# A C2f block with attention on one core: a norm in halves, parameter work reordered, one product moved, a new tail order

## The chip, the cores and the metric

The kernel runs on one core of a Trainium2 chip. The metric is the device time of one execution in microseconds (us), and the time before is the median of three runs. All arithmetic is float32.

## The reference, cut to what matters

Eight images of 512 channels and 32x32 pixels are normalized by groups, and go through one block with a residual around it.

```python
x = x + block(group_norm(x))            # 32 groups of 16 channels

def block(x):                           # cbs = silu(batch_norm(conv(.)))
    t = cbs(x, cv1)                     # 1x1, 512 -> 512
    ys = [t[:, :256], t[:, 256:]]
    for i in range(2):
        z = cbs(ys[-1], m_cv1[i])       # 3x3, 256 -> 256
        q, k, v = qkv_i(z)              # 1x1, 4 heads of 64
        z = softmax(q @ (k + r_i) / 8) @ v        # 1024 x 1024 per head
        ys.append(ys[-1] + silu(batch_norm(m_cv2[i](z))))     # 1x1
    return cbs(concat(ys), cv2)         # 1x1, 1024 -> 512
```

## The kernel before, in words

**Engines.** TensorE (PE) multiplies, ScalarE (ACT) applies functions and copies, VectorE (DVE) adds, GpSimd (POOL) does small work and issues part of the DMAs, SyncE (SP) issues the rest. Channels lie on the 128 partitions, so an image is four tiles of 128x1024 at the input and two in the inner steps. A product of 128x512 is recorded as two matmul instructions.

**Pairs.** Images are handled in four pairs (p = 0 to 3), and each pair runs in this order: the first 3x3 convolution for both images; projection and attention of image a with the weights of n = 0; m2, which is the 1x1 convolution behind the attention; projection and attention of image b; the second convolution for both; the same attentions with n = 1; and cv2, which joins all parts. While a pair is in its first two attentions, the next pair's images a and b are normalized (`group_norm`), and their cv1 is begun behind each attention (`next_cv1`: begin, go_on, sums, rest). In pair 0 the next cv1 is done directly (`direct`), with one(0) in begin, one(1) in go_on, and one(2) and one(3) in rest. In pairs 1 and 2 it is done by Strassen's scheme with seven products; rest(0) to rest(3) are four of them, made from sums t1 to t4 of the normalized input, which lie in the tiles of q and k.

**The 3x3 convolution** is done by Winograd's scheme. `tiles_in` turns an input into the tiles v on DVE (with two small memsets of w_rows on POOL in each of three passes), `conv3x3` multiplies these by filters u and turns the products back on DVE. `make_u` turns nine taps of the weights into one third of the filters in each of three groups: six DVE operations (L408 to L413) and two on ACT (L406, L407), and ahead of two groups three sums on DVE (L390 to L396). It is a generator with eight steps per filter, so that its caller can place steps between other work; each group ends with three stores to DRAM from POOL (L417). The tiles u_new come from a ring of ten slots of the tag u, which also holds loaded weights. The filters of n = 0 are made at the start, those of n = 1 in and behind the attention of the first image of pair 0: (0,0) inside it, then (0,1), (1,0) and (1,1). Their taps were all read into the tiles Y2[0] and Y2[1].

**Attention** (`attention_fast`): for each of four groups (two heads times half the queries), eight blocks of keys. l_ps (L957) are the logits, pt (L961) their exponentials on ACT, acc (L975, L977) their sum on DVE, av_ps (L991) the product with v. Two blocks make a slot; `behind` holds what is issued behind slot (g, at), where plain g stands for (g, 0), `NG` for the end of the last group, and NG + 1 for what follows it. `hooks` fills it: a step of the norm where the slot is in NORM_A (image a) or NORM_B (image b), a filter step where its number is in `us`. The sums of exp are inverted to scale the output. Usually they go through DRAM to be turned and spread (`sums`, `spread`, `scale`). With `at_once` the last group's are kept in PSUM by `last_sums` (L1025), inverted on DVE over 128x512 (L1108), and only a check goes through DRAM.

**The group norm** takes statistics (L653, L654), averages them over groups on PE (`gn_mean`: gm, dev; `gn_rstd`: gr, L679), makes gr and shift on POOL (L680, L736, L737) and applies them on ACT (L741), one whole tile at a step. The first pair's norms are `group_norm_part`, with the statistics on ACT for the later ones (L694, L721).

**Parameter work on POOL.** `make_r` sums the two position vectors into r_new (L206) and stores it (L210), `make_sq` makes the Strassen sums of the projection weights on DVE and stores seven blocks from POOL (L237), `keep_y` stores the cv1 output (L1439, L1440). For n = 1 make_r and make_sq are asked for behind slots (1, 2) and (3, 2) of the first attention.

**Order.** The order in the program isn't the order on an engine. A planner in the framework places each instruction in its engine's queue by its own costs when its inputs and buffers are there, and so may bring it far forward. `with tc.issue_after(i)` sets the instructions of its block that run on the engine of i behind i, and has no effect on other engines. PSUM has three accumulators of the tag `big` and one of `av`.

**The tail.** The last image ends with `cv2`: half of its products were made earlier (`parts`), DVE adds the new half (L1415), ACT applies silu (L460), DVE adds the input x_res (L1418), and the result is stored (L1420).

## Time and profile before

| | us |
|---|---|
| median of three runs (2348.94 to 2358.16) | 2351.87 |
| profiled execution, its own time | 2352.97 |
| its span | 2351.5 |
| PE busy in the span | 2231.2 |
| DVE busy | 1745.9 |
| ACT busy | 1085.3 |
| POOL busy | 229.6 |
| PE's mean granted clock | 0.987 |

All times in the profile count from the span's start. Busy time says how long an engine had an instruction in work, not that the work was needed then. A gap before an instruction is written as [us <- what ended it]; a wait for several things is put down to the last of them. Slices or stretches of the span show which engine is the bound there.

### The profile page before, as it was taken

How to read it: one execution, taken by the hardware profiler on the slowest of the kernel's cores; microseconds unless marked ns; L12 is line 12 of the kernel's file. 1: busy time of each engine (PE TensorE's matmuls, PEld its weight loads, DVE VectorE, ACT ScalarE, POOL GpSimd, SP SyncE). 2: the span in 40 equal slices, each digit the busy share in tenths (PEclk: the TensorE clock that was granted, in tenths of full speed). 3: DMA queues.
4: the chain of work that ended last, by engine and by line, in shares of the span. 5: the costliest groups of instructions: out<-in, count | busy, mean ns of one | idle time of the engine just before them, and what ended most of it. 6: DMA issues, size and time to landing. Idle time of an engine off the chain costs nothing.

```text
span 2351.5 us, 40448 instructions
## 1 busy us (share of the span) xinstructions
PE 2231.2 (95%) x16338; PEld 1083.4 (46%) x16338; DVE 1745.9 (74%) x2630; ACT 1085.3 (46%) x1321; POOL 229.6 (10%) x426
## 2 busy tenths in 40 slices
PE   7798899999999999999999999999999999999997
PEld 3553336533456343744347443564344733473443
DVE  6978677858938778986866868887794867786642
ACT  7245362546224665355422575545622454335532
POOL 4302200010020000000022000000002000000002
PEclk9899899999999999999999999999999999999998
DMA  9522715331266042612158132442126611151114
GB/s 330 205 76 100 286 37 195 126 118 46 69 184 220 25 166 66 213 59 91 38 134 257 60 117 88 131 158 73 55 64 172 225 43 59 59 192 37 51 32 127
DMA packets 128068, 281.31 MB, mean 120 GB/s; under 512 B 34144, under 2 KB 55376, under 8 KB 126848
## 3 DMA queue, kind: packets, MB, share of 16 engines
q1 hardware_dynamic: 99888, 192.50, 24.9%
q0 software_dynamic: 27984, 86.13, 12.0%
q8 instruction: 131, 2.15, 0.4%
q14 instruction: 65, 0.53, 0.1%
HBM read 210.55 MB, written 68.03 MB: 118 GB/s over the span
## 4 chain that ended last, share of the span: by engine, by line
PE 58%; issue 16%; DVE 14%; DMA 4%; ACT 2%; POOL 1%; SPq 0%; DVEq 0%; ACTq 0%; POOLq 0%
PE av_ps L991 13%; PE l_ps L957 12%; PE c L1209 7%; PE c_new L1209 5%; PE m_ps L1189 4%; PE p_ps L847 4%; PE ps L486 3%; PE c_ps L603 3%; PE x_ps L1309 3%; DVE acc L977 2%; PE pv_ps L853 2%; ACT pt L961 1%; PE s_ps L1008 1%; DMA rs<-r_dram 1%; DVE c_e L611 1%
## 5 line engine op out<-in xcount | busy, mean ns | idle before, releaser
L961 ACT ACTIVATE pt<-l_ps 128x1024 f32<-128x1024 f32 x512 | 495.6, 1023 | 348.9 <-PE l_ps L957 316.0
L977 DVE TENSOR_TENSOR acc<-acc,pt 128x1024 f32<-128x1024 f32 x384 | 471.5, 1228 | 91.9 <-ACT pt L961 68.5
L957 PE MATMUL l_ps<-q,kr 64*64 64x512 f32 x4096 | 491.2, 593 | 14.9 <-ACT pt L961 12.4
L991 PE MATMUL av_ps<-pt,vT 64*64 64x512 f32 x4096 | 488.7, 594 | 8.5 <-DVE z L999 7.5
L957 PEld LDWEIGHTS l_ps<-q,kr 64*64 64x64 f32 x4096 | 157.0, 133 | 288.3 <-issue 247.1
L991 PEld LDWEIGHTS av_ps<-pt,vT 64*64 64x64 f32 x4096 | 155.2, 134 | 285.4 <-issue 240.8
L603 PE MATMUL c_ps<-v_in,u 128*64 128x128 f32 x4320 | 240.2, 273 | 5.5 <-issue 5.5
L603 PEld LDWEIGHTS c_ps<-v_in,u 128*64 128x64 f32 x4320 | 235.8, 137 | 13.4 <-issue 13.4
L1189 PE MATMUL m_ps<-z,m_sb 128*128 128x512 f32 x256 | 114.6, 600 | 4.6 <-DVE z L1063 4.6
L847 PE MATMUL p_ps<-t_z,sq 128*128 128x512 f32 x224 | 106.7, 597 | 7.9 <-DVE c_t L610 7.9
L975 DVE TENSOR_TENSOR acc<-pt 128x1024 f32<-128x1024 f32 x64 | 79.0, 1234 | 37.2 <-ACT pt L961 37.1
L608 ACT COPY c_m<-c_ps 128x512 f32<-128x512 f32 x48 | 28.1, 585 | 168.9 <-PE c_ps L603 101.6
L460 ACT ACTIVATE t<-m_ps,bh,sh 128x512 f32<-128x512 f32 x64 | 46.8, 775 | 93.1 <-PE m_ps L1189 85.5
L847 PE MATMUL p_ps<-z,sq 128*128 128x512 f32 x168 | 80.2, 604 | 8.2 <-ACT z L460 8.2
L1259 POOL DMA_DIRECT2D c_out<-in_x_dram x56 | 50.5, 996 | 303.2 <-ACT c_out L460 301.3
L1189 PEld LDWEIGHTS m_ps<-z,m_sb 128*128 128x128 f32 x256 | 48.7, 192 | 65.1 <-issue 55.3
L521 POOL MEMSET w_rows<- 128x32 f32 x48 | 7.8, 163 | 679.1 <-PE s_ps L1008 389.8
L1063 DVE TENSOR_TENSOR z<-z,rs 128x512 f32<-128x512 f32 x64 | 43.9, 686 | 33.9 <-DMA rs<-r_dram 33.8
L486 PE MATMUL ps<-x,w 128*128 128x512 f32 x128 | 57.8, 606 | 5.9 <-ACT y_half L460 5.9
L999 DVE TENSOR_TENSOR z<-av_ps,z 128x512 f32<-128x512 f32 x64 | 43.9, 686 | 23.7 <-ACT z L998 23.7
L460 ACT ACTIVATE z<-z,bh,sh 128x512 f32<-128x512 f32 x64 | 46.9, 802 | 30.9 <-DVE z L641 29.8
L460 ACT ACTIVATE c_out<-cz,bh,sh 128x512 f32<-128x512 f32 x14 | 16.7, 1293 | 91.3 <-DVE cz L1286 91.3
(308 smaller groups left out, 3193.2 us busy)
## 6 DMA issues: line engine op xcount, KB each, us to landing
u<-u SPq DMA_DIRECT2D x135, 512.0 KB
sq<-sq SPq DMA_DIRECT2D x42, 384.0 KB
rs<-r_dram SPq DMA_DIRECT2D x120, 128.0 KB
x<-in_x_dram SPq DMA_DIRECT2D x28, 512.0 KB
r_in<-r SPq DMA_DIRECT2D x28, 512.0 KB
y_in<-y SPq DMA_DIRECT2D x28, 512.0 KB
c_out<-in_x_dram POOLq DMA_DIRECT2D x56, 256.0 KB, 5.4
out_dram<-c_out POOLq DMA_DIRECT2D x56, 256.0 KB, 3.6
```

The source lines that it names most:

```text
L460: silued[0] = nc.scalar.activation(dst, src, AF.Silu, scale=sh[:, k : k + 1], bias=bh[:, k : k + 1])
L486: last_product[0] = nc.tensor.matmul(ps[:, half, :], w_of(k), rhs_of(k, half), start=(k == begin), stop=(k == end))
L603: nc.tensor.matmul(to[o], us[cp][:, k, row, c, o], rhs, start=(k == 0), stop=(k == NM - 1),)
L847: nc.tensor.matmul(ps[:, o, :], w[:, o, :], rhs, start=not onto, stop=True, skip_group_check=onto)
L957: nc.tensor.matmul(ps[kh * HD : (kh + 1) * HD, hd, :], kr[r, c, o : o + HD], q[r, c, ts(half, HALF)], start=True, stop=True,)
L961: last_exp[0] = exp = nc.scalar.activation(pt, ps, AF.Exp, scale=SCALE)
L975: return nc.vector.tensor_tensor(accs[g], pt[0], pt[1], ALU.add)
L977: ins = nc.vector.tensor_tensor(accs[g], accs[g], pt[i], ALU.add)
L991: nc.tensor.matmul(avs[g][hd * HD : (hd + 1) * HD, kh, :], vT[r, j, o : o + HD], pt[i][r, hd, :], start=(j == 0), stop=(j == NJ - 1),)
L1189: nc.tensor.matmul(pss[oc][:, half, :], m2_sb[:, n, k, ts(oc, P)], ao[:, k, ts(half, HALF)], start=(k == 0), stop=(k == NM - 1),)
L1209: nc.tensor.matmul(ps[:, o, :], w[:, k, ts(o, P)], rhs[part][:, c], start=(k == 0 and not onto), stop=(k == KB - 1), skip_group_check=onto,)
L1309: nc.tensor.matmul(ps[:, o, :], w[:, c, ts(o, P)], rhs[c], start=(c == 0 and not onto), stop=(c == 1), skip_group_check=onto,)
```

## The change

The change edits eight places.

1. `group_norm` takes `pieces` and applies the norm to parts of a tile; image b of a pair uses 2 and a new list of slots, NORM_B. It also records the POOL instruction that makes the shift (`shifted`).
2. At the start two filter steps move behind the mean of the first image's second half, four steps instead of five stand before the second image's mean, and the later filter stores and `keep_y(0)` are set behind the second image's shift on POOL.
3. In the first attention, make_r and make_sq for n = 1 are set behind the shift of the third image on POOL, make_r one slot group later; the steps of the first filter are at other slots.
4. That attention runs with `at_once`, and go_on of the next cv1 is issued from inside it.
5. The taps of filter (0,1) are read early into Y2[1], those of (1,0) and (1,1) into tiles of the tags q and k. Sixteen filter steps are set behind the scaling on DVE, and the rest stays behind m2.
6. In pairs 1 and 2 the sum t4 of image b is in p4 and not in the tile of k, and rest(3) is issued behind the second convolution.
7. In `cv2` all the sums of a channel block are issued first, and the residual sum and store of a block are issued one block later.
8. `end.check` for the first attention follows its m2.

The diff, cut to its core:

```diff
-        def group_norm(xts):
+        def group_norm(xts, pieces=1):
...
-            nc.gpsimd.tensor_scalar(shift, shift, -1.0, None, ALU.mult)
+            shifted[0] = nc.gpsimd.tensor_scalar(shift, shift, -1.0, None, ALU.mult)
             yield
             for c in range(NX):
-                with tc.issue_after(last_exp[0].ins) if last_exp[0] else nullcontext():
-                    nc.scalar.activation(
-                        xts[c], xts[c], AF.Identity, scale=gr[:, c : c + 1], bias=shift[:, c : c + 1]
-                    )
-                yield
+                for half in range(pieces):
+                    part = xts[c][:, ts(half, HW // pieces)]
+                    with tc.issue_after(last_exp[0].ins) if last_exp[0] else nullcontext():
+                        nc.scalar.activation(
+                            part, part, AF.Identity, scale=gr[:, c : c + 1], bias=shift[:, c : c + 1]
+                        )
+                    yield
...
+            late, outs = [], []
+
+            def out_later(t, size, q, rows, has):
+                def run():
+                    with tc.issue_after(outs[-1].ins) if outs else nullcontext():
+                        outs.append(nc.vector.tensor_tensor(t, t, has[:, :size], ALU.add))
+                    q.dma_start(rows, t)
+                    residual()
+
+                return run
...
+                        added = nc.vector.tensor_tensor(part, src, part, ALU.add)
                         src = part
+                        if n == 0 and late:
+                            with tc.issue_after(added.ins):
+                                flush(1 if final else 0)
+                    srcs.append((at, size, src))
+                with tc.issue_after(added.ins) if final else nullcontext():
+                    flush()
+                for n, (at, size, src) in enumerate(srcs):
...
                     silu(from_planes(t), by_slot(src), bn_cv2 + oc)
-                    nc.vector.tensor_tensor(t, t, res[done][:, :size], ALU.add)
                     q = nc.sync if final else nc.gpsimd
-                    q.dma_start(rows_of(out, oc, at, size), t)
+                    late.append(out_later(t, size, q, rows_of(out, oc, at, size), res[done]))
...
-        chunk = make_u(0, 0, 1, areas[0, 0, 1], first_units)
-        for _ in range(2):
-            made = next(chunk)
     first = begin(Y_ORDER[0], [0])
     with tc.issue_after(first.ins), tc.issue_after(made.ins):
         averaged = next(norm)
+    chunk = make_u(0, 0, 1, areas[0, 0, 1], first_units)
+    with tc.issue_after(averaged.ins):
+        for _ in range(2):
+            made = next(chunk)
...
-    with tc.issue_after(averaged.ins), tc.issue_after(shifted.ins):
+    with tc.issue_after(made.ins), tc.issue_after(shifted.ins):
         nc.vector.tensor_scalar(rstd, bnp[:, :, 3], BN_EPS, None, ALU.add)
...
     with tc.issue_after(made.ins):
-        for _ in range(5):
+        for _ in range(4):
             made = next(chunk)
...
-    with tc.issue_after(averaged.ins):
+    with tc.issue_after(averaged.ins), tc.issue_after(shifted.ins):
         for made in chunk:
             pass
...
-    keep_y(0, y0s, Y1[0])
+    with tc.issue_after(shifted.ins):
+        keep_y(0, y0s, Y1[0])
...
+        def t_qk_p():
+            if len(pairs_of_t) == 1:
+                pairs_of_t.clear()
+                return held("p4")
+            return t_qk()
...
-            f = s.strassen_cv1(take_blocks("sw", None, which, SW_NAMES), xts, y0s, y1, t_qk)
+            f = s.strassen_cv1(take_blocks("sw", None, which, SW_NAMES), xts, y0s, y1, t_qk_p if which else t_qk)
...
         def filters(keys):
-            for oc, k, at in keys:
-                yield from make_u(1, oc, k, load_raw(1, oc, k, Y2[at]))
+            for oc, k, area in keys:
+                yield from make_u(1, oc, k, area)
+
+        def load_late(oc, k, area):
+            nc.gpsimd.dma_start(
+                area[:, : 9 * P].rearrange("p (t o) -> p t o", o=P), m_cv1_w[1, ts(k, P), :, ts(oc, P)]
+            )
+            return area
+
+        def late_area(tag):
+            return act.tile([P, 2 * HW], F32, tag=tag, name="taps_late")
...
-        NORM_B = ((0, 2), (0, 3), (1, 2), (1, 3), 2, (2, 1), (2, 2), (2, 3))
+        NORM_B = ((0, 1), (0, 2), (0, 3), (1, 1), 2, (2, 1), (2, 2), (2, 3), 3, (3, 1), (3, 2), (3, 3))
         if p == 0:
-            more_u = filters([(0, 0, 0)])
-        behind = hooks(NORM_A, range(0, 16, 2)) | {NG: begin_cv1(0, Y1[0], ia + 2)}
+            more_u = filters([(0, 0, load_late(0, 0, inside(Y2[0])))])
+            second_taps = load_late(0, 1, inside(Y2[1]))
+        behind = hooks(NORM_A, (0, 1, 4, 10, 11, 12, 13, 14)) | {NG: begin_cv1(0, Y1[0], ia + 2)}
...
+            def with_r():
+                with tc.issue_after(s.shifted[0].ins):
+                    make_r(1, raw_1)
+                first()
+
+            behind[2, 1] = with_r
+
+            def with_sq():
+                before()
+                with tc.issue_after(s.shifted[0].ins):
+                    make_sq(1, q_tiles, [t[:, j] for t in q_sums for j in range(2)])
+
+            behind[3, 2] = with_sq
+        if p == 0:
+            behind[NG + 1] = lambda: nxt.go_on()
+        end = s.attention_fast(qkv, z[:, :, 0], at_of(ia, 0), behind, at_once=p == 0)
...
-                more_u = filters([(0, 1, 1), (1, 0, 1), (1, 1, 1)])
-                end.sums()
-                nxt.go_on()
-                end.spread()
-                with tc.issue_after(end.added.ins):
-                    for _ in range(5):
-                        made = step_u()
-                with tc.issue_after(made.ins):
-                    end.scale()
-                    for _ in range(7):
+                more_u = filters(
+                    [(0, 1, second_taps)] + [(1, k, load_late(1, k, late_area(tag))) for k, tag in enumerate("qk")]
+                )
+                with tc.issue_after(end.scaled.ins):
+                    for _ in range(16):
                         made = step_u()
                 last = m2_a()
-                with tc.issue_after(made.ins):
-                    for _ in range(3):
-                        made = step_u()
+                end.check()
...
-            norm = s.group_norm(xs)
+            norm = s.group_norm(xs, 2)
...
-            for i in range(4):
+            for i in range(4 if direct else 3):
                 nxt.rest(i)
...
         t = s.conv3x3(1, vs, u_of(1), z, summed=z[:, :, 0])
+        if more and not direct:
+            nxt.rest(3)
```

More of the change, by code (lines that the diff above doesn't have):

```diff
@@ L463, in silu @@
             return silued[0]
+        shifted = [None]
         silu_in, last_product, silued, last_exp, m2_silu = [], [None], [None], [None], [None]
@@ L1404, in cv2, with flush @@
             done = 0
+            late, outs = [], []
[6 more added lines that the diff above has]
+                return run
+            def flush(n=0):
+                while len(late) > n:
+                    late.pop(0)()
             for oc in range(NO):
@@ L1407, in cv2 @@
                 ps = cv2_products(w_of, rhs_of, oc, ks, ends=(ks[0], ks[-1]), by_half=oc == NO - 1)
+                final = parts and oc == NO - 1
+                srcs = []
+                added = None
                 for n, size in enumerate(sizes(oc)):
-                    _, at, _ = places[done]
-                    final = parts and oc == NO - 1
-                    t = act.tile([P, HALF], F32, tag=("h", "h", "rs")[n] if final else "h", name="t", bufs=4 if final and n == 2 else 2)[:, :size]
+                    at = sum(sizes(oc)[:n])
                     src = ps[:, at // HALF, at % HALF : at % HALF + size]
@@ L1414, in cv2 @@
                         part = parts[oc][:, at : at + size]
-                        nc.vector.tensor_tensor(part, src, part, ALU.add)
+                        added = nc.vector.tensor_tensor(part, src, part, ALU.add)
                         src = part
+                        if n == 0 and late:
[5 more added lines that the diff above has]
+                for n, (at, size, src) in enumerate(srcs):
+                    tag = ("h", "h", "rs")[n] if final else "h"
+                    t = act.tile([P, HALF], F32, tag=tag, name="t", bufs=4 if tag == "rs" else 2)[:, :size]
                     silu(from_planes(t), by_slot(src), bn_cv2 + oc)
-                    nc.vector.tensor_tensor(t, t, res[done][:, :size], ALU.add)
                     q = nc.sync if final else nc.gpsimd
-                    q.dma_start(rows_of(out, oc, at, size), t)
+                    late.append(out_later(t, size, q, rows_of(out, oc, at, size), res[done]))
                     done += 1
-                    residual()
+                if not parts:
+                    flush()
+            flush()
         return SimpleNamespace(**locals())
@@ L1668 @@
             before = behind[3, 2]
-            first = behind[1, 2]
+            first = behind[2, 1]
             raw_1 = load_r(1)
-            behind[1, 2] = lambda: (first(), make_r(1, raw_1))
-            behind[3, 2] = lambda: (before(), make_sq(1, q_tiles, [t[:, j] for t in q_sums for j in range(2)]))
-        end = s.attention_fast(qkv, z[:, :, 0], at_of(ia, 0), behind)
+            def with_r():
[11 more added lines that the diff above has]
+        end = s.attention_fast(qkv, z[:, :, 0], at_of(ia, 0), behind, at_once=p == 0)
         for made in more_u:
```

## The prediction

> **What bounds the kernel now.** I read the page first, then busy times over chosen stretches, then the timeline wherever a stretch showed idle TensorE time. Page, sections 1 and 2:

> ```profile
> PE 2231.2 (95%) x16338; PEld 1083.4 (46%) x16338; DVE 1745.9 (74%) x2630; ACT 1085.3 (46%) x1321; POOL 229.6 (10%) x426
> PEclk9899899999999999999999999999999999999998
> ```

> TensorE (PE) is the bound: 95% busy, so all that can be had without removing matmuls is 2351.5 - 2231.2 = 120 us of idle time, plus what it loses at a lowered clock. The change removes no matmul of weight, so it is priced by gaps. Stretches (us; busy time of PE, PEld, DVE, ACT, POOL with counts; clock; DMA share; GB/s):

> ```profile
> 64.00:83.30 19.30, 15.26 (x38) 6.52 (x37) 14.84 (x29) 6.82 (x6) 15.85 (x16) 1.00 0.58 208
> 83.30:107.80 24.50, 12.50 (x162) 12.08 (x163) 24.19 (x50) 1.17 (x2) 1.78 (x8) 0.80 0.59 210
> 107.80:137.90 30.10, 29.10 (x426) 26.29 (x426) 29.92 (x60) 5.99 (x10) 0.55 (x1) 0.93 0.51 172
> 155.80:221.90 66.10, 59.81 (x546) 21.16 (x545) 52.43 (x76) 42.20 (x51) 6.67 (x12) 0.97 0.11 39
> 221.90:257.90 36.00, 25.52 (x62) 10.36 (x59) 23.27 (x56) 9.47 (x17) 17.31 (x29) 0.82 0.78 267
> 291.80:354.60 62.80, 58.15 (x546) 20.17 (x545) 48.00 (x60) 40.16 (x45) 4.04 (x8) 1.00 0.14 51
> 752.50:810.60 58.10, 57.63 (x546) 21.49 (x545) 49.68 (x65) 39.16 (x44) 3.68 (x5) 1.00 0.10 26
> 861.10:924.90 63.80, 58.44 (x546) 20.16 (x545) 56.01 (x75) 39.37 (x44) 4.04 (x8) 1.00 0.12 39
> ```

> The reader is to see three stages. From 83.3 to 137.9 (first convolution) VectorE (DVE) is busy 54.1 of 54.6 us: what delays DVE before it delays everything. From 221.9 to 257.9 (after the first attention) PE is idle 10.5 us at clock 0.82. And the second image's attention under which the next norm runs takes 62.8 us (pair 0) and 63.8 us (pair 1), against 58.1 us for the first image's in pair 1, with the same matmuls; pair 2's is 63.1.

> The timeline says what ends those waits. Before the first convolution:

> ```profile
> 55.72 2.80 DVE L408 TENSOR_TENSOR u_new<-taps 128x256 f32<-128x256 f32 x1 [2.15 <-DMA u<-u_new]
> 56.16 2.06 POOL L206 TENSOR_TENSOR r_new<-rw_sb,rh_sb 128x512 f32<-128x512 f32 x2
> 65.39 11.00 POOL L206 TENSOR_TENSOR r_new<-rw_sb,rh_sb 128x512 f32<-128x512 f32 x2
> 78.95 0.69 DVE L548 TENSOR_TENSOR w_d<-w_rows 128x512 f32<-128x512 f32 x1 [4.46 <-POOL w_rows L521]
> ```

> GpSimd (POOL) builds r_new here though the program asks for it in the first attention; a DVE operation of 0.42 us takes 2.80, and DVE waits 4.46 us for a memset queued behind r_new and four DMA issues. After the first attention:

> ```profile
> 247.68 2.08 PE L486 MATMUL ps<-x,w 128*128 128x512 f32 x2 [5.87 <-ACT y_half L460]
> 253.62 0.69 DVE L1063 TENSOR_TENSOR z<-z,rs 128x512 f32<-128x512 f32 x1 [3.08 <-DMA rs<-r_dram]
> 254.36 3.78 PE L1189 MATMUL m_ps<-z,m_sb 128*128 128x512 f32 x4 [4.60 <-DVE z L1063]
> ```

> m2 stops half way until the last softmax sums have gone through DRAM and back. And in the second image's attention (alike at 901 to 908 and 1460 to 1467):

> ```profile
> 331.27 0.15 DVE L679 TENSOR_SCALAR gr<-gv_ps 128x4 f32<-128x4 f32 x1
> 334.61 2.37 ACT L741 ACTIVATE x<-x,shift,gr 128x1024 f32<-128x1024 f32 x2 [5.02 <-POOL shift L737]
> 337.94 1.09 PE L957 MATMUL l_ps<-q,kr 64*64 64x512 f32 x8 [2.80 <-ACT pt L961]
> ```

> gr is read late, ScalarE (ACT) waits 5.02 us for the shift with an exponential queued behind, runs two whole-tile norms, and PE waits.

> [...]

> **Part A, start-up.** The parameter-sum blocks (make_r, make_sq) are tied behind the third image's shift on POOL, so four r_new, their four stores and the early sq stores leave 55 to 80 us. That takes away the 4.46 wait and the stretch, 2.80 - 0.42 = 2.4. Moving two filter steps behind the mean lets gm be copied when the first filter ends, about 21.4 instead of 23.05 (12 filter operations of 0.42 started every 0.34 had shared that time), and PE restarts 1.6 us sooner. The rstd wait of 2.1 us at 27.9 shrinks too. But filter buffers still wait for stores (3.3 us until 48.7, 2.2 until 55.7) with DMA at 0.81 to 1.05 of its time, and these waits take back early arrival: I count 1.1. One filter step fewer before the second image's mean and keep_y behind its shift take its norm forward from 50.6; PE ends the first image at 51.0 and had 0.48 us to wait, so nothing more. Sum 4.5 + 2.4 + 1.1 = **8 us off**, all on DVE's path. Bounds: 3 (the memset's wait alone, partly) and 11 (the store waits shrink as well).

> **Part B, first attention and after.** make_r now runs in the attention at (2,1): four r_new of 1.04 us, four stores of 0.55 us, then memsets and filter stores queued behind on POOL; seven sq issues follow at (3,2). DVE has 66.1 - 52.4 = 13.7 us free there, and filter steps leave slots 5 to 9, where the mean waited (2.0 us at 187). A blocked POOL costs up to 4 x 1 us of DVE: **0**, bounds 4 either way.

> After it, at_once replaces the trip through DRAM by eight s_ps matmuls (1.09 us at L1025), two row copies (0.57 each), an add (0.69), a reciprocal of 128x512 (3.35, L1108) and the scale (0.69). one(1) goes ahead as before. The second image of this pair already has this order: one(0) at 354.60, m2 done at 376.5, 22 us. Today's 36.0 become 22.0: 14 us. s_ps is done at 230, scaling at about 236, m2 starts near 237, so the reciprocal hides behind one(1) (7.1 us). The last-total DMA and its 0.16 us add hide behind m2.

> What comes next: all filter work of (0,1), (1,0), (1,1) is tied behind the scale. One filter takes 9.6 us of DVE (a group of 2.1, two of about 3.75), three 28.8, with four m2 sums of 0.69: 236 + 31.6 = 268. The last two lie in q and k, so kr can't be written earlier. Its product would be ready at 221.9 + 22 + 13.9 (two more products) + 3.4 = 261. PE goes on with q and v products in the other two accumulators for about 7 us (L817 takes 7.07 for all v), which covers most of it; I charge 3. The two raw loads (7.0 us landed at 233.9) start once logits have released q and k, some 14 us before needed. Ends: nothing charged, or 8 with DMA (0.78 and 0.80 now from 222 to 292) near full: **11 off**, bounds 14 and 6.

> **Part C, the norm by halves.** In three attentions rstd moves from (1,3) to (1,1): three slots of about 3.6 us before the first norm, where there was one. Eight norms of half a tile, one per slot (about 0.72 us each by L721), replace four of 1.24 in four slots; 8 x 0.72 - 4 x 1.24 = 0.8 us more on ACT, in slots with two exponentials of 0.97, so 2.7 of 3.6 us. At the 58.1 us of an attention with its norm in order: 4.7 + 5.7 + 5.0 = 15.4. But pair 1 already has 56.0 us of DVE work, 96% of 58.1, so not all: **11 off**, bounds 14 and 4.

> **Part D, one product behind the second convolution** (pairs 1 and 2). It takes 3.43 us of PE. That convolution is DVE's: from 944.3 to 997.3 DVE has no gap, PE waits 1.1 and 1.2 us at its end. DVE's work stays, so nothing is won; the product takes an accumulator that the next projection used, freed only at 994 to 995. t4 in p4 moves no work. **1 lost** in all, bounds 0 and 3.

> **Part E, the tail.** Sums of the parts no longer wait behind ACT; output adds come one channel block later. But silu waits for a buffer whose output DMA takes up to 5.9 us, and that remains:

> ```profile
> 2327.70 1.31 ACT L460 ACTIVATE t<-part,bh,sh 128x512 f32<-128x512 f32 x1 [11.14 <-DMA out_dram<-t]
> 2332.84 1.28 DVE L1415 TENSOR_TENSOR part<-ps,part 128x512 f32<-128x512 f32 x2
> ```

> Stepping the last four silus forward by these waits ends between 2339 and 2342.3, as now: **1 off**, bounds 3 off and 1 lost.

> **Sum**: -8 + 0 - 11 - 11 + 1 - 1 = -30 against the profiled execution's own 2352.97 (span 2351.5), so 2323; the median of the runs is 1.1 lower, hence 2322. All good ends give -46, all bad ends -5.

> **Rivals.** First: DVE becomes the bound where PE's gaps close. For: 96% in part C, 31.6 us of filters in one go. Against: today's gaps end on other engines. A gives 6, B 5, C 6, the rest 0: 17 off, 2335. Second: the norm change does little, because the gr read stays behind the tile transforms of g = 1 on DVE (it came after nine of them at 331.27). C gives 3, total 22 off: 2330. Third, slower: k is filled and read too late. The ring has ten slots, four held by weights, so two filter groups are in flight; if each group waits for its stores (4.7 us at start-up, issue 51.04, buffer taken 55.72) nine groups take 9 x (3.9 + 4.7) = 77 us and kr waits until 313, 49 us past the forecast's 264: 2371. It decides from 264 on: the gain is gone at 294. Against: at 261 to 273 groups ran through without such a wait.

> **Chances.** Forecast 0.69, first rival 0.16, second 0.09, third 0.06. A measurement of this kernel can tell about 0.5%, 12 us, from no change: faster means below 2340. The first rival straddles that a little: faster 0.87, same 0.07, slower 0.06. The range reaches from nearly all good ends (2304) past the first rival (2341).

> **What would show it.** No r_new before the first attention and no w_rows wait at 79; first attention starting near 148 instead of 155.8; 22 to 25 us from its end to m2's end, with clock near 1; a kr write that PE waits for less than 4 us; second images' attentions at 58 to 60 us without the 2.8 us gap; a convolution no shorter in pairs 1 and 2. An attention still at 63, or kr later than 20 us after m2, would make it wrong.

## The result, and the profile after

The changed kernel takes 2347.7 us (median of 13 runs, 2343.4 to 2351.9), the kernel before in the same comparison 2354.8 us (2348.9 to 2359.3). The ratio is 0.9968, with a 95% interval of 0.9958 to 0.9979: 7 us faster, where 30 were forecast, and outside the range. The profiled execution took 2349.4 us, its span is 2348.0 us, 3.5 less than before. Page of the changed kernel, sections 1 and 2:

```profile
PE 2237.3 (95%) x16338; PEld 1089.6 (46%) x16338; DVE 1748.5 (74%) x2632; ACT 1089.3 (46%) x1334; POOL 224.8 (10%) x426
PEclk9899999999999999999999999999999999999998
```

PE is busy 6 us longer with the same 16338 matmuls: idle time fell by almost 10 us, and most of that came back as busy time of the same matmuls. Part of it is the clock: the time at half clock, up to PE's last matmul, is 54.6 us in this profile and 47.8 in that of before. The clock's dip in the fifth slice, after the first attention, has gone; single stretches further on ran at 0.95 to 0.97, too short to show in a slice. Busy time over stretches of the changed kernel (us; PE, PEld, DVE, ACT, POOL with counts; clock; DMA share; GB/s). They are, in this order: from the first attention's end to the end of its m2; from there to the second image's attention; that attention in pair 0, in pair 1 and in pair 3:

```profile
219.30:241.40 22.10, 22.10 (x61) 9.51 (x58) 11.88 (x21) 6.22 (x7) 7.02 (x13) 1.00 0.57 186
241.40:281.00 39.60, 35.01 (x96) 17.61 (x94) 38.30 (x92) 16.83 (x29) 15.90 (x30) 1.00 0.91 333
281.00:343.30 62.30, 59.54 (x546) 21.42 (x545) 48.76 (x61) 41.11 (x49) 5.23 (x8) 0.97 0.24 88
850.10:913.00 62.90, 58.12 (x547) 21.09 (x545) 55.05 (x74) 40.11 (x48) 5.23 (x8) 1.00 0.13 43
1950.40:2016.10 65.70, 60.09 (x539) 20.30 (x538) 57.13 (x73) 35.19 (x40) 3.46 (x8) 0.97 0.16 55
```

The same view of the kernel before, for two stretches that the prediction did not look at, the one behind m2 and the second image's attention of pair 3:

```profile
258.10:291.80 33.70, 33.70 (x95) 17.66 (x93) 25.49 (x53) 12.87 (x18) 7.55 (x14) 0.99 0.81 303
1954.90:2018.80 63.90, 58.28 (x538) 19.76 (x537) 57.00 (x73) 35.19 (x40) 3.45 (x8) 1.00 0.16 55
```

Three things are to be seen. The stage that at_once was to shorten is 22.1 us instead of 36.0; the forecast was 22.0. The stretch behind it grew from 33.7 to 39.6 us, with DVE now busy 38.3 of it. And the second images' attentions are as long as they were. Pair 3 has no next pair, so no norm runs there; its attention takes 63.9 us before and 65.7 after, like those with a norm.

Laid end to end (each number is a stretch of PE's timeline, after less before): the first attention starts 3.7 us earlier (152.0 instead of 155.8) and takes 1.1 longer; the stage to the end of m2 -14.2; the stretch behind it +6.0; the second image's attention -0.6. At 343 us the kernel is 11.4 ahead. From there it loses 9.0: 3.9 around the moved product (two pairs), 2.1 and 1.7 in the second images' attentions of pairs 2 and 3, 1.3 and 1.1 in the first convolutions of pairs 1 and 3, whose code is the same, less 1.1 elsewhere. Those convolutions take 31.7 to 32.1 us (pair 1) and 31.7 to 33.3 us (pair 3) in the ten experiments below, against 34.0 and 32.9 here and 32.8 and 31.9 before, so their part is scatter between executions. The tail gains 1.2: from PE's last matmul to the end of the span 16.2 us instead of 17.3.

The waits themselves, first at the start-up (timeline of the changed kernel; start, length, engine, line, operation, and in brackets the idle time before it with what ended it):

```profile
37.80 0.38 PE L661 MATMUL gm_ps<-mv,gmat 64*64 64x4 f32 x4 [2.45 <-DVE mv L700]
57.78 0.43 DVE L408 TENSOR_TENSOR u_new<-taps 128x256 f32<-128x256 f32 x1 [3.78 <-ACT y_half L460]
63.70 0.42 DVE L413 SCALAR_TENSOR_TENSOR u_new<-taps,u_new 128x256 f32<-128x256 f32 x1
```

PE's wait for the mean at 37.80 was 0.56 us before. The last start-up filter operation begins at 63.7 as before (63.8), although r_new has left POOL: a wait of 3.78 us ahead of a filter operation, which the profile puts down to a silu on ACT, stands where 2.15 and a stretched operation stood. Only the 4.46 us for the memset are gone.

Behind m2 (the same view):

```profile
260.27 0.42 ACT L406 ACTIVATE u_new<-taps_late 128x256 f32<-128x256 f32 x1 [6.52 <-DVE taps_late L396]
261.50 2.21 ACT L460 ACTIVATE ypad<-ps,bh,sh 128x512 f32<-128x512 f32 x2
263.76 3.72 PE L820 MATMUL p_ps<-w_qkv,z 128*128 128x256 f32 x16 [1.80 <-ACT ypad L460]
267.51 0.42 ACT L406 ACTIVATE u_new<-taps_late 128x256 f32<-128x256 f32 x1 [2.29 <-DVE taps_late L392]
268.12 1.00 ACT L803 COPY q<-ps 128x1024 f32<-128x1024 f32 x1
269.18 3.72 PE L820 MATMUL p_ps<-w_qkv,z 128*128 128x256 f32 x16 [1.70 <-ACT q L803]
273.99 2.41 PE L487 MATMUL ps<-z,w_qkv 128*128 128x512 f32 x5 [1.09 <-ACT vT L824]
274.83 1.22 DVE L808 TENSOR_TENSOR kr<-ps,rw_sb 128x1024 f32<-128x1024 f32 x1
```

ACT stands 6.52 us at a filter copy that needs DVE, with cv1's silu behind it, and PE waits for the accumulator that this silu frees. The copy of q that PE waits for next stands behind another filter copy, one that waited 2.29 us for DVE. PE is idle 1.80 + 1.70 + 1.09 = 4.6 us in this stretch, each time behind ACT, and was never idle in it before; these are 4.6 of the 6.0. kr comes at 274.8, not by 264 to 268.

And the attentions of second images (PE, the same view; pair 1, then pair 3):

```profile
868.75 0.23 PE L661 MATMUL gm_ps<-mv,gmat 64*64 64x4 f32 x2 [2.82 <-DVE mv L655]
...
1972.22 0.64 PE L1011 MATMUL s_ps<-acc,ones 128*32 128x256 f32 x8 [2.20 <-DVE acc L980]
2003.87 0.64 PE L1011 MATMUL s_ps<-acc,ones 128*32 128x256 f32 x8 [0.95 <-DVE acc L980]
2005.51 1.95 PE L994 MATMUL av_ps<-pt,vT 64*64 64x512 f32 x16 [1.01 <-DVE z L1002]
```

The waits for ACT and gr have gone in pair 1, and PE waits 2.82 us for the mean's own input instead. Without a norm it waits for acc.

### The profile page after: what moved, and what is told of

Its sections match the earlier page's. It is cut to its first block, busy times and chain, and to the rows that moved or that the text cites. A ratio compares the mean times of both kernels' runs of the same rounds, so it can differ in the third digit from the quotient of the medians.

```text
span 2348.0 us, 40464 instructions
## 1 busy us (share of the span) xinstructions
PE 2237.3 (95%) x16338; PEld 1089.6 (46%) x16338; DVE 1748.5 (74%) x2632; ACT 1089.3 (46%) x1334; POOL 224.8 (10%) x426
## 3 DMA queue, kind: packets, MB, share of 16 engines
q8 instruction: 131, 2.15, 0.4%
## 4 chain that ended last, share of the span: by engine, by line
PE 71%; DVE 17%; issue 4%; DMA 2%; ACT 2%; POOL 0%; SPq 0%; DVEq 0%; ACTq 0%; POOLq 0%
PE av_ps L994 15%; PE l_ps L960 14%; PE c L1212 8%; PE c_ps L604 7%; PE c_new L1212 6%; PE p_ps L850 5%; PE m_ps L1192 4%; PE x_ps L1312 4%; PE ps L487 3%; DVE acc L980 3%; PE pv_ps L856 2%; PE s_ps L1011 1%; PE p_ps L856 1%; DVE acc L978 1%; ACT pt L964 1%
## 5 line engine op out<-in xcount | busy, mean ns | idle before, releaser
L994 PE MATMUL av_ps<-pt,vT 64*64 64x512 f32 x4096 | 494.9, 601 | 11.6 <-DVE z L1002 10.5
L460 ACT ACTIVATE t<-m_ps,bh,sh 128x512 f32<-128x512 f32 x64 | 46.8, 775 | 85.6 <-PE m_ps L1192 78.0
L460 ACT ACTIVATE z<-z,bh,sh 128x512 f32<-128x512 f32 x64 | 46.9, 804 | 27.5 <-DVE z L642 26.8
L460 ACT ACTIVATE c_out<-cz,bh,sh 128x512 f32<-128x512 f32 x14 | 16.7, 1292 | 91.6 <-DVE cz L1289 91.6
L850 PEld LDWEIGHTS p_ps<-t_z,sq 128*128 128x128 f32 x224 | 38.9, 190 | 38.7 <-issue 29.9
```

Of the source, the lines that this page charges most:

```text
L460: silued[0] = nc.scalar.activation(dst, src, AF.Silu, scale=sh[:, k : k + 1], bias=bh[:, k : k + 1])
L850: nc.tensor.matmul(ps[:, o, :], w[:, o, :], rhs, start=not onto, stop=True, skip_group_check=onto)
L994: nc.tensor.matmul(avs[g][hd * HD : (hd + 1) * HD, kh, :], vT[r, j, o : o + HD], pt[i][r, hd, :], start=(j == 0), stop=(j == NJ - 1),)
```

## The experiments

My theory after this: the norm never made those attentions long, tile transforms on DVE did; the start-up's new order and the moved product cost time; behind m2 the silus queue behind filter copies. The tile transforms are `tiles_in` of image a's output, made in three passes; `tiles_later` puts pass 1 ahead of image b's attention and pass 2 at the start of its group 1 (g = 1), some 7 us of DVE work each. The rival in each case is that the forecast's mechanism was right and chance or a lowered clock hid it. Every ratio below is to the kernel before, run beside it.

**The product ahead of the second convolution again.**

```diff
-    f = s.strassen_cv1(..., t_qk_p if which else t_qk)
+    f = s.strassen_cv1(..., t_qk)
-            for i in range(4 if direct else 3):
+            for i in range(4):
-        if more and not direct:
-            nxt.rest(3)
```

> The changed kernel with all four rest products of pairs 1 and 2 ahead of the second convolution again, and t4 in the tile of k. Theory (that convolution is bound by DVE and starts early for nothing, the product then comes on top): from the end of the second image's m2 to the start of the next attention 68.1 us again instead of 70.1 in both pairs, the convolution 33.2 us instead of 37.1, and the whole 4 us below the changed kernel's 2347.7, so 2343.7. Rival (the 2 us per pair are a lowered clock or chance, not the product): 70.1 us stays and the whole is 2347.7 within 1 us.

2344.5 us, ratio 0.9961 (0.9947 to 0.9974). Both intervals from m2 to the next attention are 68.1 us. Stretches of the convolution in pair 1, this kernel:

```profile
943.70:976.90 33.20, 32.07 (x578) 31.48 (x577) 32.99 (x68) 8.32 (x12) 0.23 (x2) 1.00 0.71 230
```

and the changed kernel:

```profile
942.30:979.40 37.10, 33.78 (x577) 33.18 (x577) 36.77 (x75) 7.93 (x12) 0.23 (x2) 0.95 0.66 213
```

With the product ahead, the convolution starts 3 us later after m2, runs at full clock with DVE busy throughout, and ends 0.9 us sooner after m2 than with the product gone (46.9 instead of 47.8). In the changed kernel the product then comes on top: from there to the next attention 22.2 us instead of 21.2. The product behind costs 1.97 us in each pair.

That a lowered clock made the difference is excluded by a later run that also has the product behind, the one with the start-up's old order below. From the end of m2 to the next attention it took 69.8 us in both pairs, at full clock; in pair 1:

```profile
929.40:999.20 69.80, 65.17 (x693) 48.55 (x691) 60.57 (x116) 26.39 (x34) 0.45 (x4) 1.00 0.57 189
```

So 1.7 us per pair belong to the product's place; the other 0.3 came together with a lowered clock. The theory holds. In the medians this run alone is not clear of the changed kernel, as the two intervals overlap.

**The norm in whole tiles at the old slots.**

```diff
-        NORM_B = ((0, 1), (0, 2), (0, 3), (1, 1), 2, ..., (3, 3))
+        NORM_B = ((0, 2), (0, 3), (1, 2), (1, 3), 2, (2, 1), (2, 2), (2, 3))
-            norm = s.group_norm(xs, 2)
+            norm = s.group_norm(xs)
```

> The changed kernel with the second image's norm in whole tiles and in the old slots. Theory (the second images' attentions are long because of the tile transforms on DVE, and the earlier mean only put one wait in the place of another): attentions of the second images in pairs 0, 1, 2 at 62.8, 63.8 and 63.2 us, in pair 3, which has no norm, 64 us; the whole 2347.7 within 2 us. Rival (the halves do save the ACT waits, 2 us or more in each of the three, and a lowered clock hid it in the profile): the whole 2353 or more.

2347.3 us, ratio 0.9973 (0.9962 to 0.9984); attentions 62.8, 63.6, 62.8 and 63.9 us. The halved norm, as a whole, is worth nothing that shows. By pairs that is a gain and a loss: with it, four other profiles with the same code take 60.6 us in pair 0 (62.8 before, 62.2 in the changed kernel's own profile, with a stretch at half clock), and six take 64.3 to 65.3 in pair 1 (before: 63.8). In one of the six, the kernel with both reversals below, a wait of 2.82 us for mv is followed there by a stretch at half clock, and the mean clock of that attention is 0.97.

**The tile transforms taken out of these attentions.**

```diff
-        tiles_later(1)
-        behind = hooks(NORM_B, (), {1: lambda: tiles_later(2)}) | {
+        behind = hooks(NORM_B) | {
...
-        s.tiles_in(Y2[0], putter(vs, 0), [0])
+            s.tiles_in(Y2[0], putter(vs, 0))      # with those of the second image
```

> The changed kernel with the tile transforms of passes 1 and 2 of the first image's output (about 14 us of DVE work in each pair) made behind the second image's attention instead of under it, without their way through DRAM. Theory (this DVE work is what makes the second images' attentions long): all four fall to 58 to 59.5 us, that of pair 3 too, the waits for acc, for z and for mv on PE go, and the second convolution starts some 10 us later after each, so the whole is 25 to 40 us longer. Rival (the norm makes them long): pairs 0 to 2 stay at 62 to 65 us, and only pair 3, without a norm, changes.

The attentions take 58.5, 59.9, 59.9 and 57.6 us. In pairs 1 and 3:

```profile
863.30:923.10 59.80, 57.75 (x546) 21.08 (x545) 47.23 (x59) 39.86 (x48) 3.29 (x3) 1.00 0.08 24
1992.00:2049.60 57.60, 57.60 (x538) 19.63 (x537) 44.53 (x48) 35.16 (x40) 0.00 (x0) 1.00 0.09 30
```

Pair 3 runs without a gap, so its excess of 6 us went with the tile work. The attentions of pairs 1 and 2 stay 2.3 us above pair 3's: that, and not 5, is what the norm costs there when the tile work is away. Two of the four are 0.4 above what I expected, and the wait for mv stays (2.05 us in pair 1): I had it go with the tiles, wrongly. The whole takes 2398.3 us (one run), 50 more than the changed kernel, not 25 to 40. The edit also moves pass 0 behind m2, and from m2 to the next attention each pair takes 18 to 19 us longer where I expected some 10; in pair 0 DVE is busy 79 of these 87 us.

**The start-up's old order, with make_r still behind the third image's shift.**

```diff
     with tc.issue_after(made.ins):
         for made in chunk:
             pass
+        chunk = make_u(0, 0, 1, areas[0, 0, 1], first_units)
+        for _ in range(2):
+            made = next(chunk)
...
-        for _ in range(4):
+        for _ in range(5):
             made = next(chunk)
...
-    with tc.issue_after(averaged.ins), tc.issue_after(shifted.ins):
+    with tc.issue_after(averaged.ins):
...
-    with tc.issue_after(shifted.ins):
-        keep_y(0, y0s, Y1[0])
+    keep_y(0, y0s, Y1[0])
```

> The changed kernel with the start-up's filter steps and norm in the order of before, and make_r and make_sq still behind the third image's shift. Theory (the new order gave nothing: the filters end at 64.0 us in both kernels, and only the memset's wait of 4.5 us went, by make_r leaving POOL): the first attention starts at 149 to 152 us, no later than the changed kernel's 152.0, and the whole is 2347.7 less 0 to 3. Rival (the new order did win its part, and without it that is lost): the first attention starts at 153.5 or later, the whole 2349 or more.

2345.4 us, ratio 0.9963 (0.9954 to 0.9973). Timeline, the last start-up filter and the first logits:

```profile
61.05 0.42 DVE L413 SCALAR_TENSOR_TENSOR u_new<-taps,u_new 128x256 f32<-128x256 f32 x1
...
148.50 1.09 PE L960 MATMUL l_ps<-q,kr 64*64 64x512 f32 x8
```

The filters end 2.7 us earlier than in both other kernels, and the first attention starts 7.3 us before that of the kernel before. Moving make_r and make_sq off POOL is worth 7.3 us; the new order takes 3.5 of them back. These are single profiles. Over all of them the first attention starts at 150.2 to 152.8 us in the four kernels with the whole new order and at 148.5 to 149.6 in the six with the old one, 2.6 us apart in the mean. The intervals of this run and of the changed kernel overlap.

**Both reversals at once**, the base of all that follows.

> The changed kernel with both reversals at once: the rest products ahead of the second convolution (alone 3.2 us below the changed kernel in the medians) and the start-up's old order with make_r still late (alone 2.3 below). Theory (they lie in different stages and add up): 2342 within 1.5 us, first attention from 148.5 us. Rival (they share a gain, or those runs were lucky): 2344.5 or more.

2338.7 us, ratio 0.9932 (0.9918 to 0.9945): they add up. The median lies below the 2340.5 to 2343.5 that I expected from the two medians, and near what the traces say, 3.9 + 3.5 below the changed kernel. This interval is clear of the changed kernel's.

**Half of the start-up's new order left in** (four filter steps ahead of the second image's mean, later filter stores and keep_y behind its shift).

> The two reversals, but with the second half of the start-up's new order left in: four filter steps instead of five ahead of the second image's mean, the later filter stores and keep_y behind that image's shift. The steps ahead of the first image's second mean are as before. Theory (the second image's earlier norm puts its ACT work ahead of the filters' ACT copies, and DVE then waits 3.8 us for u_new, as in the changed kernel): first attention at 151.5 to 152.5 us, the whole 2 to 4 us above the two reversals. Rival (the mean taken ahead of two filter steps is what costs, by making the second image's squares and their mean 2 us later): first attention at 148 to 149.5 us, the whole as with the two reversals.

2341.0 us, ratio 0.9938 (0.9922 to 0.9954); first attention at 150.1 us. That lies between the two expectations, and just below the 150.2 to 152.8 of the whole new order. One profile within such a scatter does not show how the cost divides between the two halves; that stays open.

**The mean two slots later.**

```diff
-NORM_B = ((0, 1), (0, 2), (0, 3), (1, 1), 2, ...)
+NORM_B = ((0, 2), (0, 3), (1, 1), (1, 3), 2, ...)
```

> The two reversals, and the halved norm of the second image with its mean two slots later, at (1,1), and rstd at (1,3), in the three pairs that have it. Theory (tile transforms on DVE bound these attentions, and the wait for mv only shows where that is paid): attentions of the second images in pairs 0 to 2 still 61 to 65 us, the whole as with the two reversals within 1.5 us. Rival (the wait of 2.2 to 2.8 us for mv is a price of its own, put there by the early mean): these three fall by 2 us or more each, to 60 to 61 us, the whole 5 to 7 us lower.

2338.7 us, as with the two reversals; ratio 0.9926 (0.9912 to 0.9939). Attentions 61.1, 62.0 and 61.1 us. The wait for mv in pair 1 is gone, and one of 1.95 us for the exponentials on ACT has come. In these profiled executions the attentions of pairs 1 and 2 are 2.3 and 1.1 us shorter than the base's (1.7 of the 2.3 is the stretch at half clock behind the wait for mv, which the base has), but other stretches with the same code were longer, and the median doesn't show it. A gain of a few us isn't excluded by the interval.

**kr ahead of tile pass 1, and silus ahead of filter copies, in pair 0.**

```diff
-                    for _ in range(16):
+                    for _ in range(13):
                         made = step_u()
...
-                with tc.issue_after(made.ins), tc.issue_after(last.ins):
+                with tc.issue_after(made.ins), tc.issue_after(last.ins), tc.issue_after(s.silued[0].ins):
                     for made in more_u:
...
+        with tc.issue_after(s.kr_added[-2].ins) if direct else nullcontext():
             tiles_later(1)
```

> The two reversals, and in pair 0 after m2 the ACT copies of the last filters set behind the next cv1's silus, and tile pass 1 of the first image set behind the first kr sum on DVE. Theory (the time given back after m2 comes from silus queued behind filter copies on ACT, and from tile pass 1, 7.3 us of DVE that my sum did not count ahead of kr): from the end of m2 to the second image's attention 34 to 37 us where the start-up run had 41.3 and the changed kernel 39.7; the attention behind it grows by up to 3 us because it now holds tile pass 1; the whole 1 to 5 us below the two reversals. Rival (the filters' own DVE work and the lowered clock set that stretch): 39 us or more, and the whole the same or higher.

2339.3 us, ratio 0.9940 (0.9926 to 0.9953). From m2 to the attention 37.7 us instead of the base's 41.2, 0.7 above the expected span and below the rival's 39; the attention takes 62.4 instead of 60.6. PE's timeline of the v products, in the base:

```profile
262.25 9.13 PE L820 MATMUL p_ps<-w_qkv,z 128*128 128x256 f32 x32 [3.35 <-ACT ypad L460]
```

and here:

```profile
258.94 3.62 PE L820 MATMUL p_ps<-w_qkv,z 128*128 128x256 f32 x16
264.11 3.72 PE L820 MATMUL p_ps<-w_qkv,z 128*128 128x256 f32 x16 [1.56 <-ACT q L803]
```

The wait for the silu is gone, and so is a second price of it: after 3.35 us of waiting the 32 instructions took 9.1 us instead of 7.3. The granted clock was 0.50 in the base for 3.4 us of that time:

```profile
262.97:266.39 3.42, 3.42 (x9) 2.70 (x9) 3.42 (x9) 1.13 (x4) 1.14 (x3) 0.50 0.99 384
```

But the whole did not fall by 1 to 5 as expected: of the 3.5 us, 1.8 came back in the attention behind, which now holds tile pass 1, and the median does not show the rest.

**The two tile passes at two group boundaries.** A group named in late_acc starts its sum on DVE later, so that a tile pass can stand at its boundary.

```diff
-        tiles_later(1)
-        {1: lambda: tiles_later(2)}
+        {1: lambda: tiles_later(1), 2: lambda: tiles_later(2)}
-                if j0 == 0 and g == 1:
+                if j0 == 0 and g in late_acc:      # (1, 2)
                     accs[g] = None
```

> The two reversals, and in all second images' attentions tile pass 1 at the boundary before group 1 and pass 2 at that before group 2, instead of pass 1 ahead of the attention and pass 2 before group 1; the accumulating sum of group 2 starts late too, as that of group 1 did. No work is added or taken away. Theory (the tile passes cost because two bursts of 7 us of DVE fall within one group, not by their sum): the four attentions fall to 59.5 to 62 us, that of pair 3 from 63.9 to 61.5 or less, the whole 5 to 12 us below the two reversals. Rival (DVE's sum of work is the bound, wherever it lies): 62 to 65 us stay, the whole within 2 us or higher.

2336.9 us, ratio 0.9922 (0.9908 to 0.9935). Attentions 58.9, 60.3, 62.0 and 58.0 us: pair 3 comes down to 58.0 with the same work, from 65.6 in the base and 63.9 in the run before it. But the whole fell by only 1.8, in the rival's band. In pairs 1 and 2 the time comes back behind the attention, from its end to the convolution 36.7 us instead of 32.2 in each. In pair 2 (PE):

```profile
1475.14 1.09 PE L1028 MATMUL s_ps<-acc,ones 64*64 64x512 f32 x8 [2.70 <-DVE acc L980]
```

DVE ends the last group's sum late, because the next cv1's sums (t_x) now meet the tail of the tile work. So both are true: in pair 3 the place of the bursts decides, in pairs 1 and 2 DVE's work in all.

The run also tests tile pass 1 as a cause behind m2 in pair 0, since it takes it out of that stretch:

```profile
237.70:280.50 42.80, 37.99 (x97) 19.57 (x95) 34.78 (x80) 16.94 (x29) 14.76 (x28) 0.92 0.91 332
```

DVE has 34.8 us of work there instead of the base's 38.7, and the stretch is no shorter (42.8 us instead of 41.2). It has two stretches of 3.4 us at half clock and the base one; taking off half of each, both come to some 39.5 us, by my estimate.

**What the experiments point to:** the reversals, the boundaries in pairs 0 and 3 alone, and the silus ahead of the filter copies.

```diff
+        apart = direct or not more
+        if not apart:
             tiles_later(1)
+        {1: lambda: tiles_later(1), 2: lambda: tiles_later(2)} if apart else {1: lambda: tiles_later(2)}
+        late_acc=(1, 2) if apart else (1,)
```

> The two reversals, the tile passes at the boundaries before groups 1 and 2 in pairs 0 and 3 alone (pairs 1 and 2 as changed), and the last filters' ACT copies behind the next cv1's silus. Theory (in pairs 1 and 2 the gain under the attention was paid back behind it, in pair 3 not; and after m2 in pair 0 the silus behind filter copies hold PE): pair 3's attention at 58 us and its second convolution no later relative to it; pair 0 from the end of m2 to the second image's attention 36 to 39 us where the two reversals had 41.3, its attention 59 to 61; the whole 2329 to 2334. Rival (the accumulator wait only moves to kr, which comes behind all filters in any order): 41 us or more stay in pair 0, the whole 2335 or more.

2330.9 us, ratio 0.9893 (0.9877 to 0.9909): it beats both kernels, 24 us below the one before. The stretch behind m2 in pair 0, and pair 3's attention:

```profile
238.00:275.30 37.30, 34.81 (x96) 17.72 (x95) 34.63 (x80) 17.00 (x29) 14.69 (x28) 1.00 0.88 320
1935.00:1993.00 58.00, 57.61 (x538) 19.66 (x538) 52.84 (x70) 35.20 (x40) 3.69 (x10) 1.00 0.16 56
```

37.3 and 58.0 us as expected, pair 3's convolution is no later behind its attention (35.7 us, as in the base), and pair 0's attention takes 59.3. DVE does 52.8 us of work in 58.0 without holding PE up. Behind m2 this kernel differs from the run before it in two things only, the silus ahead of the filter copies and 13 filter steps instead of 16 in the group behind the scaling; the two were not tested apart. PE still waits 1.34 us there for kr.

## Why the prediction was wrong, point by point

**Part A, 8 forecast, 3.7 found.** Right: the memset's wait and the stretched operation, 6.9 us, were make_r's doing (7.3 in the run with the old order). Its four r_new, which took 1.04 to 9.99 us each on POOL in the start-up before, take 1.05 to 1.06 in the changed kernel's first attention; from 196.7 to 201.8, beside three of them, two sums of acc on DVE take 5.08 us where one alone takes 1.23. Failed: the two sentences on the new order, "PE restarts 1.6 us sooner" within 1.1 gained, and the norm taken forward, "so nothing more". I asked of the moved steps what they would free, not what then waits: PE waits 2.45 us for the mean of the next norm at 37.8, DVE 3.78 us at 57.8. The order cost 3.5 in these profiles, and 2.6 in the mean of all.

**Part B, 11 forecast, about 8 found.** The 14 was right (14.2), and the first attention's 0 within its bounds (+1.1). The mis-sized term is "I charge 3": it was 6.0. I had counted the filters' DVE time and had the v products cover the late kr. Left out were the filters' ACT copies, which hold cv1's silus and the copies of q and v, and so the accumulators: PE's 4.6 us of new idle time all end on ACT, none on kr. With the silus ahead the stretch is 37.3 to 37.7 us. Tile pass 1, 7.3 us of DVE work that the planner put among the filters, was left out of the sum as well, but taking it away alone shortened nothing. In the changed kernel's trace the silu at 261.50 runs right behind four filter copies, the first of which waited 6.52 us. I had counted such a wait on ACT for the norm, with an exponential queued behind it, and none for the filters.

**Part C, 11 forecast, nothing found.** The failed step is "at the 58.1 us of an attention with its norm in order: 4.7 + 5.7 + 5.0 = 15.4". It took the first image's attention as the measure and gave the whole excess to the norm. The control was in the profile: pair 3's second image, without a norm, takes 63.9. Most of the excess was tile work: without it the four attentions take 57.6 to 59.9. My sentence that pair 1 "already has 56.0 us of DVE work" pointed at it, and I let it take off 4 of 15. The second rival saw the size (3) but blamed the gr read.

**Part D, 1 lost forecast, 3.9 found.** The mechanism was right, DVE's work stays and nothing is won. The size was not: the step that failed is "1 lost in all", which charged half a microsecond per pair for a product of 3.43 without naming what covers the rest. It costs 1.7 at full clock and 2.0 here.

**Part E, 1 forecast, 1.2 found.** The range's lower end, 2304, lay just below all good ends together, 2352 - 46 = 2306.

The third rival, kr at 313, did not come: kr was 7 to 11 us later than forecast, not 49.

The rest, 2.1 and 1.7 us in two attentions, was in no part of the forecast. In pair 3 it is no cost of the change: both profiled executions have the same waits of PE, and the changed one ran at clock 0.97. In pair 2 the changed one has two stretches of 3.4 us at half clock, from 1430 and from 1464, and the one before has one. The first follows a wait of 2.19 us for mv, so that the early mean has a part in it. Pair 3's attention took 63.9 us in five of the profiled kernels that leave its code alone and 65.5 to 65.6 in four. Such a difference is in the two profiled spans, which differ by 3.5 us where the medians differ by 7.

## What to carry to other kernels

Before a stage's excess is put down to one piece of work, look for a repetition of the stage that lacks this piece: it is a control that costs nothing. When steps are moved or packed closer, walk every engine's queue at the new place, with the small copies too, and ask who stands behind each that waits. And work taken from one stretch of a busy engine is won only if the next stretch has room for what it displaces. Before 2 us between two profiles are explained, look at the clock in that stretch, and at the same stretch in other profiles.

## What was not expected of the hardware

```profile
1969.46:1972.87 3.41, 1.21 (x20) 0.27 (x16) 3.25 (x4) 1.84 (x2) 0.00 (x0) 1.00 0.00 0
1972.87:1976.28 3.41, 3.41 (x20) 1.07 (x24) 3.20 (x3) 0.37 (x1) 0.00 (x0) 0.50 0.03 2
```

In the kernel before, the same wait is shared by two stretches, and the clock stays up:

```profile
1971.98:1975.40 3.42, 2.50 (x24) 0.61 (x16) 3.11 (x4) 3.42 (x5) 0.00 (x0) 1.00 0.00 0
1975.40:1978.81 3.41, 2.13 (x24) 0.85 (x28) 3.31 (x4) 0.72 (x2) 0.00 (x0) 1.00 0.00 0
```

Half of 3.41 is 1.7 us, the difference between 63.9 and 65.6. From the clock's first record (16.1 us before, 17.0 after) to PE's last matmul the clock falls 8 times in the profile before and 12 times in that of the changed kernel. Ahead of each of the 20 falls lies a stretch in which PE was busy 1.55 us or less of the 3.41; in each of the 1305 stretches at full clock that another at full clock followed it was busy 1.56 us or more. The wait of 2.20 us left 1.21 us in one stretch; shared by two, it left 2.50 and 2.13.
